# A four-layer graph network: layer 0 as the maximum of two rank-one terms, its denominator on TensorE, and half-row exponentials in layer 3

## The chip, the cores and the metric

The kernel runs on one core of a Trainium2 chip. The metric is the device time in microseconds (us), the median of three runs for the kernel before: 1418.75 us (1417.5 to 1420.33). PE is TensorE, DVE VectorE, ACT ScalarE, POOL GpSimd, SP the engine whose queue starts most of the transfers.

## The reference

There are N = 2708 nodes with 128 features each, and a dense 0/1 adjacency `adj` with ones on its diagonal. Four layers follow one another, each `x = x + layer(relu(layernorm(x)))`.

- Layer 0 (attention): `H = h W^T`; each node has two scores, `src` and `dst`; `Tau = adj^T * exp(max(0.2 C, C))` with `C = src[j] + dst[i]`; rows of `Tau` are divided by their sum; `Z = (adj^T * att) H`.
- Layer 1: normalised aggregation with `adj + I`, then a weight and a Relu.
- Layer 2: mean aggregation with `adj^T`, two weights, batch normalisation over the nodes, Relu.
- Layer 3 (attention over a dense product): `den = exp(leaky_relu(s_row + s_col))`, `num = adj den`, `att = den / num`, `H = adj (att XW)`.

All is float32.

## The kernel before, in words

The nodes are cut into T = 22 tiles of 128 rows, the last with 20. A row of 2708 columns is worked in two halves of 1354 (`HALF`) and, on PE, in six blocks of about 452 (`BLK`)[...]. Six banks (`acc_bank`) hold accumulators; two more (`bank`) go round for everything else.

Layer 0 (L212 to L261). The layernorm, the transposes (`relu_transposed`), a row of the `dst` scores spread over all partitions (`spread_row` into `row_a`, a plain copy) and the projection (`project` into `hs`, whose column 128 is the `src` score) come first. Then, for each tile and half, ACT adds the tile's score to the row (L228) and sums the row of the adjacency for the degree (L229), DVE forms the leaky maximum (L230), ACT takes the exponential (L231), DVE multiplies by the adjacency (L232, `tau`) and once more (L237, `at2`), POOL adds `tau` into `row_b` (L236), and PE aggregates `at2` into the six accumulators (L240). After the loop 22 small products against ones (L249) turn `row_b` into the denominator; the accumulators are copied out (`evacuate`), transposed, and added to `xs` scaled by its reciprocal (L258, L259).

Layers 1 and 2 (L274 to L345) stream the adjacency, transposed or not, through PE (`aggregate`, L192).

Layer 3 sorts the nodes by score and works in NS = 42 steps of 128 rows (L676 to L694). In a step three gathers on POOL's queue bring rows and values (`fetch`, L653); DVE forms the exponent `e` (L681); for each of the six blocks PE forms the product `num` (L685), ACT its logarithm (L686); DVE subtracts it from `e` in three pieces, after blocks 2, 4 and 5 (L688); one exponential over the whole row follows (L690). PE then adds the step before into the accumulators (`spread_values`, L674). `num` has only the two rotating banks; `e` and `ln` have two buffers.

The program is not ordered by hand. A planner writes the queue of each engine ahead of time, from the order of the program as priority and its own model of which instruction is ready; on the chip each engine then runs its queue in that order. What loads an activation table on ACT is placed afterwards, where the queue needs another table. Buffers of a pool are handed on when their last reader is done: four for the streamed adjacency, two for `z`, `tau` and `at2`.

At entry, ACT's queue starts the loads of `x` (one transfer of 1344 KB and a tail), then five weights, then eight vectors of 128 values, each scattered one value to a partition (`vecs`); SP's queue starts the adjacency.

Of the kernel before, what the change touches and what calls it, by code (L numbers as in the profile page):

```python
# [8 lines left out]
F32 = mybir.dt.float32  # L9
BF16 = mybir.dt.bfloat16  # L10
I32 = mybir.dt.int32
AF = mybir.ActivationFunctionType
# [5 lines left out]
def kernel(  # L18
# [19 lines left out]
    nc = tc.nc  # L38
# [11 lines left out]
    NB = len(BLK)  # L50
    NSTREAM, NKEEP = 4, 3

    def rows(t):
        return min(P, N - t * P)

    def cols(t):
        return slice(t * P, (t + 1) * P)

    def vcols(t):
        return slice(t * P, t * P + rows(t))  # L60
# [8 lines left out]
    def bank():  # L69
        return ps.tile([P, 512], F32, tag="bank", name="bank")  # L70

    def acc_bank(b):
        return ps_acc.tile([P, 512], F32, tag=f"acc{b}", name=f"acc{b}")
# [1 line left out]

    xs = big.tile([P, T, D], F32, name="xs")
    nc.vector.memset(xs[:, TF:, :], 0.0)
    nc.scalar.dma_start(xs[:, :TF, :], x[: TF * P, :].rearrange("(t p) d -> p t d", p=P))
    nc.scalar.dma_start(xs[:TAIL, TF, :], x[TF * P :, :])

    ident = const.tile([P, P], F32, name="ident")
    make_identity(nc, ident)
# [6 lines left out]
    def load(name, shape, src):  # L89
        t = const.tile(shape, F32, name=name)  # L90
        nc.scalar.dma_start(t, src)
        return t
# [3 lines left out]
    wn_sb = load("wn_sb", [P, P], w_n)  # L96
    wc_sb = load("wc_sb", [P, P], w_c)
    w3_sb = load("w3_sb", [P, P], w3)
    vecs = const.tile([P, 8], F32, name="vecs")
    for i, v in enumerate((att_src[0], att_dst[0], a3[0, :P], a3[0, P:], b_n, b_c, gamma, beta)):  # L100
        nc.scalar.dma_start(vecs[:, i : i + 1], v.rearrange("(p o) -> p o", o=1))

    def transposed(name, w):
        p = bank()
# [70 lines left out]
    def spread_row(dst, lhsT):  # L175

        for c in range(0, NPAD, 512):
            n = min(512, NPAD - c)
            p = bank()
            nc.tensor.matmul(p[:, :n], lhsT, hT[:, c : c + n], start=True, stop=True)  # L180
            nc.scalar.copy(dst[:, c : c + n], p[:, :n])

    def evacuate(b, acc):
        lo, hi = BLK[b]
# [11 lines left out]
    with tc.tile_pool(name="stream", bufs=NSTREAM) as stream, tc.tile_pool(name="keep", bufs=1) as keep, tc.tile_pool(  # L196
# [12 lines left out]
            return a  # L209


        layernorm()  # L212
        relu_transposed()
        spread_row(row_a, w0_spread[:, 1, :])
        project(w0_ext)
        deg2 = const.tile([P, T, 2], F32, name="deg2")
        nc.gpsimd.memset(deg2, 0.0)
        accs = [acc_bank(b) for b in range(NB)]
        for t in range(T):
            r = rows(t)  # L220
            a = load_rows(adj, t)
            for h in range(2):
                c = slice(h * HALF, (h + 1) * HALF)
                z = edge.tile([P, HALF], F32, tag="z", name="z")
                tau = edge.tile([P, HALF], F32, tag="tau", name="tau")
                at2 = edge.tile([P, HALF], F32, tag="at2", name="at2")
                junk = edge.tile([P, HALF], F32, tag="junk", name="junk", bufs=1)
                nc.scalar.activation(z[:r], row_a[:r, c], AF.Identity, bias=hs[:r, t, P : P + 1])  # L228
                nc.scalar.activation(junk[:r], a[:r, c], AF.Identity, accum_out=deg2[:r, t, h : h + 1])  # L229
                nc.vector.scalar_tensor_tensor(z[:r], z[:r], 0.2, z[:r], ALU.mult, ALU.max)  # L230
                nc.scalar.activation(z[:r], z[:r], AF.Exp)  # L231
                nc.vector.tensor_mul(tau[:r], a[:r, c], z[:r])  # L232
                if t == 0:
                    nc.gpsimd.tensor_copy(row_b[:, c], tau)
                else:
                    nc.gpsimd.tensor_add(row_b[:r, c], row_b[:r, c], tau[:r])  # L236
                nc.vector.tensor_mul(at2[:r], a[:r, c], tau[:r])  # L237
                for b in range(3 * h, 3 * h + 3):
                    lo, hi = BLK[b]
                    nc.tensor.matmul(  # L240
                        accs[b][:, : hi - lo],
                        hs[:r, t, :P],
                        at2[:r, lo - h * HALF : hi - h * HALF],
                        start=(t == 0),
                        stop=(t == T - 1),
                    )
        den = bank()
        for t in range(T):
            nc.tensor.matmul(den[: rows(t), t : t + 1], row_b[:, vcols(t)], ones[:, 0:1], start=True, stop=True)  # L249
        rden = small.tile([P, T], F32, tag="rden", name="rden")  # L250
        nc.vector.reciprocal(rden[:, :TF], den[:, :TF])
        nc.vector.reciprocal(rden[:TAIL, TF:], den[:TAIL, TF:T])
        for b in range(NB):
            evacuate(b, accs[b])
        for t in range(T):
            r = rows(t)
            p = bank()
            nc.tensor.transpose(p[:, :P], yT[:, cols(t)], ident)  # L258
            nc.vector.scalar_tensor_tensor(  # L259
                xs[:r, t, :], p[:r, :P], rden[:r, t : t + 1], xs[:r, t, :], ALU.mult, ALU.add  # L260
            )  # L261

        deg = const.tile([P, T], F32, name="deg")
        nc.vector.tensor_add(deg, deg2[:, :, 0], deg2[:, :, 1])
        deg1 = const.tile([P, T], F32, name="deg1")
        nc.vector.tensor_scalar_add(deg1, deg, 1.0)
        dis = const.tile([P, T], F32, name="dis")
# [55 lines left out]
        nc.vector.tensor_reduce(tot[:, 0:1], sums[:, 0, :], AX.X, ALU.add)  # L323
        nc.vector.tensor_scalar_mul(tot[:, 1:2], tot[:, 0:1], -1.0 / N)
        for b, (lo, hi) in enumerate(BLK):
            junk = edge.tile([P, HALF], F32, tag="junk", name="junk", bufs=1)
            nc.scalar.activation(
                junk[:, : hi - lo],
                row_b[:, lo:hi],
                AF.Square,  # L330
                bias=tot[:, 1:2],
                accum_out=sums[:, 1, b : b + 1],
            )
# [316 lines left out]
    with tc.tile_pool(name="att", bufs=2) as attp:  # L650

        def gather(out, src, idx):
            nc.gpsimd.indirect_dma_start(  # L653
                out=out,
                out_offset=None,
                in_=src,
                in_offset=bass.IndirectOffsetOnAxis(ap=idx, axis=0),
            )

        accs = [acc_bank(b) for b in range(NB)]  # L660
        done = {}

        def fetch(s):
            a = steps.tile([P, N], F32, tag="rows", name="rows")
            gather(a[:CH, :], adj_t[:, :], row_i[:CH, s : s + 1])
            gather(a[CH:, :], pre_d[:, :], pre_i[0:2, s : s + 1])
            xw = attp.tile([P, P], F32, tag="xw", name="xw", bufs=4)
            gather(xw, xw_d[:, :], xw_i[:, s : s + 1])
            return a, xw

        def spread_values(s):
            xw, e = done.pop(s)
            for b, (lo, hi) in enumerate(BLK):
                nc.tensor.matmul(accs[b][:, : hi - lo], xw, e[:, lo:hi], start=(s == 0), stop=(s == NS - 1))  # L674

        for s in range(NS):  # L676
            a, xw = fetch(s)
            nc.vector.tensor_scalar_mul(xw, xw, c_exp[:, s : s + 1])
            e = attp.tile([P, N], F32, tag="e", name="e")
            ln = attp.tile([P, N], F32, tag="ln", name="ln")  # L680
            nc.vector.tensor_scalar(e, row_a[:, :N], c_rel[:, s : s + 1], 0.0, ALU.add, ALU.max)  # L681
            beg = 0
            for b, (lo, hi) in enumerate(BLK):
                num = bank()
                nc.tensor.matmul(num[:, : hi - lo], dmat[:, s, :], a[:, lo:hi], start=True, stop=True)  # L685
                nc.scalar.activation(ln[:, lo:hi], num[:, : hi - lo], AF.Ln, bias=tiny)  # L686
                if b in (2, 4, 5):
                    nc.vector.tensor_sub(e[:, beg:hi], e[:, beg:hi], ln[:, beg:hi])  # L688
                    beg = hi
            nc.scalar.activation(e, e, AF.Exp)  # L690
            done[s] = (xw, e)
            if s:
                spread_values(s - 1)
        spread_values(NS - 1)  # L694
        for b in range(NB):
            evacuate(b, accs[b])


        scale = small.tile([P, T], F32, tag="scale", name="scale")
        nc.vector.scalar_tensor_tensor(scale, deg, 0.0, r_exp, ALU.not_equal, ALU.mult)  # L700
        for t0 in range(0, T, 4):
            n = min(4, T - t0)
            p = bank()
            for t in range(t0, t0 + n):
                nc.tensor.transpose(p[:, cols(t - t0)], yT[:, cols(t)], ident)
            for t in range(t0, t0 + n):
                nc.vector.tensor_scalar_mul(hn[:, t, :], p[:, cols(t - t0)], scale[:, t : t + 1])


        accs = [acc_bank(b) for b in range(NB)]  # L710
        for t in range(T):
            r = rows(t)
            a = stream_rows(adj_t, t)
            aggregate(t, hn[:r, t, :], a[:r], accs)
        for b in range(NB):
            evacuate(b, accs[b])
# [38 lines left out]
```

## Time and profile before

| | us |
|---|---|
| median of three runs | 1418.75 |
| the profiled execution | 1420.33 |
| its span, first to last instruction | 1418.5 |
| PE busy in the span | 1118.0 |
| DVE busy | 756.3 |
| ACT busy | 608.5 |
| POOL busy | 397.0 |
| layer 0, first to last aggregation on PE (L240) | 61.37 to 375.4 |
| layer 3 loop, about | 870 to 1292 |

The profile is of one execution. A line of a group reads: line, engine, operation, output<-inputs, shape, count, then the busy time in us and the mean of one in ns, then the time that the engine stood before these instructions and what released it. A line of the order of time reads: start, duration, engine, line, operation, and in brackets the idle time ahead of it. A line of a window reads: window, its length, busy time of PE, PEld (weight loads), DVE, ACT, POOL with counts, the granted TensorE clock as a share of full speed, the DMA engines' busy share, and GB/s.

### The profile page before, as it was taken

What the parts mean: (1) busy time and instruction counts of PE and PEld (TensorE: products, weight loads), DVE (VectorE), ACT (ScalarE), POOL (GpSimd) and SP (SyncE); (2) the same over time, 40 slices, a digit from 0 to 9 for tenths busy, and PEclk for the clock granted to TensorE, in tenths of its full rate; (3) what the DMA queues carried; (4) which work ended last, traced back from release to release, by engine and by line L of the source; (5) the groups of instructions that cost most, each with busy time, mean ns of one, the idle gap of its engine ahead of it and who ended that gap; (6) DMA issues with size and microseconds to landing.
All of it is one profiled execution on the core that took longest, in us unless ns stands there. A gap on an engine that the chain in (4) does not pass through costs nothing.

```text
span 1418.5 us, 8891 instructions
## 1 busy us (share of the span) xinstructions
PE 1118.0 (79%) x3090; PEld 539.9 (38%) x3090; DVE 756.3 (53%) x1078; ACT 608.5 (43%) x692; POOL 397.0 (28%) x191
## 2 busy tenths in 40 slices
PE   1644445454779988997668894999999999999998
PEld 1322222122534554543424441444444444444453
DVE  3699999999630052003595483445444555454002
ACT  2656565643000040003100014888888888885000
POOL 1265656565210001000100004454545444430000
PEclk9977777767579978996698897999999999999997
DMA  8123232321048734833102865334343544452882
GB/s 289 40 78 117 78 118 78 118 78 39 0 145 301 270 112 165 307 116 157 41 1 88 351 248 202 114 134 162 126 162 130 176 146 149 139 162 106 299 307 79
DMA packets 33210, 210.26 MB, mean 148 GB/s; under 512 B 6734, under 2 KB 13182, under 8 KB 14526
## 3 DMA queue, kind: packets, MB, share of 16 engines
q1 hardware_dynamic: 18336, 145.55, 28.1%
q0 software_dynamic: 9408, 61.00, 12.9%
q10 hardware_dynamic: 5422, 3.16, 0.8%
q8 instruction: 24, 0.39, 0.1%
q14 instruction: 20, 0.16, 0.0%
HBM read 206.38 MB, written 3.30 MB: 148 GB/s over the span
## 4 chain that ended last, share of the span: by engine, by line
PE 36%; issue 17%; POOL 14%; DVE 9%; ACT 1%; DMA 0%; POOLq 0%; DVEq 0%; ACTq 0%
PE acc L192 22%; POOL rows L653 7%; POOL xw L653 6%; PE acc L490 3%; DVE bits L446 1%; DVE bits L448 1%; DVE at L237 1%; DVE z L230 1%; POOL rstd L140 1%; PE bank L162 1%; PE bank L289 1%; PE bank L296 1%; PE bank L622 1%; PE acc L240 1%; PE acc L674 1%
## 5 line engine op out<-in xcount | busy, mean ns | idle before, releaser
L240 PE MATMUL acc<-at,hs 128*128 128x452 f32 (+2 forms) x264 | 156.0, 759 | 148.7 <-DVE at L237 148.7
L685 PE MATMUL bank<-rows,dmat 128*128 128x452 f32 (+1 forms) x504 | 223.0, 568 | 33.7 <-ACT ln L686 19.8
L236 POOL TENSOR_TENSOR row_b<-row_b,tau 128x1354 f32<-128x1354 f32 (+1 forms) x42 | 171.8, 4108 | 126.4 <-DVE tau L232 126.4
L674 PE MATMUL acc<-e,xw 128*128 128x452 f32 (+1 forms) x504 | 198.8, 543 | 2.7 <-ACT e L690 2.7
L192 PE MATMUL acc<-a,hn 128*128 128x452 f32 (+2 forms) x492 | 191.9, 552 | 8.9 <-DVE hn L276 8.9
L688 DVE TENSOR_TENSOR e<-e,ln 128x1354 f32<-128x1354 f32 (+2 forms) x126 | 134.3, 1097 | 96.5 <-ACT ln L686 96.5
L686 ACT ACTIVATE ln<-bank,tiny 128x452 f32<-128x452 f32 (+1 forms) x252 | 156.1, 636 | 52.5 <-PE bank L685 42.0
L240 PEld LDWEIGHTS acc<-at,hs 128*128 128x128 f32 (+1 forms) x264 | 69.0, 272 | 233.8 <-DVE at L237 171.9
L237 DVE TENSOR_TENSOR at<-a,tau 128x1354 f32<-128x1354 f32 x38 | 154.3, 4099 | 0.0
L685 PEld LDWEIGHTS bank<-rows,dmat 128*128 128x128 f32 x504 | 86.2, 191 | 163.5 <-ACT ln L686 110.9
L192 PEld LDWEIGHTS acc<-a,hn 128*128 128x128 f32 (+1 forms) x492 | 94.7, 193 | 104.5 <-issue 95.1
L653 POOL DMA_INDIRECT xw<-xw_d,xw_i x42 | 89.9, 2140 | 157.7 <-PE acc L674 152.1
L674 PEld LDWEIGHTS acc<-e,xw 128*128 128x128 f32 x504 | 95.8, 190 | 99.6 <-issue 88.2
L681 DVE TENSOR_SCALAR e<-row_a,c_rel 128x2708 f32<-128x2708 f32 x42 | 68.5, 1630 | 108.9 <-PE acc L674 108.9
L653 POOL DMA_INDIRECT rows<-in_adj_t_dram,row_i x42 | 53.5, 1274 | 216.5 <-DVE z L632 165.0
L231 ACT ACTIVATE z<-z 128x1354 f32<-128x1354 f32 (+1 forms) x44 | 58.7, 1333 | 126.1 <-DVE z L230 123.0
L188 ACT COPY yT<-acc 128x452 f32<-128x452 f32 (+1 forms) x12 | 6.4, 536 | 237.3 <-PE acc L192 213.5
L690 ACT ACTIVATE e<-e 128x2708 f32<-128x2708 f32 x42 | 103.3, 2460 | 3.2 <-DVE e L688 2.7
L192 PE MATMUL acc<-rows,hn 128*128 128x452 f32 (+2 forms) x264 | 102.5, 548 | 0.1
L186 DVE COPY yT<-acc 128x452 f32<-128x452 f32 (+1 forms) x12 | 7.5, 628 | 124.1 <-PE acc L192 111.3
L140 POOL TENSOR_TENSOR rstd<-isq,neg_half 128x22 f32<-128x22 f32 x4 | 15.5, 3863 | 194.2 <-DVE isq L139 169.5
L192 PEld LDWEIGHTS acc<-rows,hn 128*128 128x128 f32 (+1 forms) x264 | 49.8, 190 | 49.2 <-issue 48.9
(225 smaller groups left out, 1197.3 us busy)
## 6 DMA issues: line engine op xcount, KB each, us to landing
rows<-in_adj_t_dram SPq DMA_DIRECT2D x42, 1354.0 KB, 6.9
a<-in_adj_dram SPq DMA_DIRECT2D x38, 1354.0 KB, 6.1
a<-in_adj_t_dram SPq DMA_DIRECT2D x21, 1354.0 KB, 7.0
keep<-in_adj_dram SPq DMA_DIRECT2D x2, 1354.0 KB, 9.2
xw_d<-hs ACTq DMA_DIRECT2D x1, 1408.0 KB
out_dram<-xs SPq DMA_DIRECT2D x21, 64.0 KB, 1.6
rows<-in_adj_t_dram,row_i POOLq DMA_INDIRECT x42
xw<-xw_d,xw_i POOLq DMA_INDIRECT x42
```

What stands on the lines that cost most here:

```text
L192: nc.tensor.matmul(accs[b][:, : hi - lo], stationary, moving[:, lo:hi], start=(t == 0), stop=(t == T - 1))
L231: nc.scalar.activation(z[:r], z[:r], AF.Exp)
L236: nc.gpsimd.tensor_add(row_b[:r, c], row_b[:r, c], tau[:r])
L237: nc.vector.tensor_mul(at2[:r], a[:r, c], tau[:r])
L240: nc.tensor.matmul(accs[b][:, : hi - lo], hs[:r, t, :P], at2[:r, lo - h * HALF : hi - h * HALF], start=(t == 0), stop=(t == T - 1),)
L653: nc.gpsimd.indirect_dma_start(out=out, out_offset=None, in_=src, in_offset=bass.IndirectOffsetOnAxis(ap=idx, axis=0),)
L674: nc.tensor.matmul(accs[b][:, : hi - lo], xw, e[:, lo:hi], start=(s == 0), stop=(s == NS - 1))
L681: nc.vector.tensor_scalar(e, row_a[:, :N], c_rel[:, s : s + 1], 0.0, ALU.add, ALU.max)
L685: nc.tensor.matmul(num[:, : hi - lo], dmat[:, s, :], a[:, lo:hi], start=True, stop=True)
L686: nc.scalar.activation(ln[:, lo:hi], num[:, : hi - lo], AF.Ln, bias=tiny)
L688: nc.vector.tensor_sub(e[:, beg:hi], e[:, beg:hi], ln[:, beg:hi])
L690: nc.scalar.activation(e, e, AF.Exp)
```

## The change

1. `x` is loaded in three pieces of seven tiles and a tail on SP's queue, ahead of the adjacency. The eight vectors go as rows of one tile (`vrow`), which PE transposes into `vecs`.
2. In layer 0, `exp(max(0.2 C, C))` divided by `exp(dst)`, which the normalisation cancels, is `max(e^src, e^(0.2 src) * e^(-0.8 dst))`. `spread_row` now stores `exp(-0.8 dst)`, and one Relu with a scale and a bias of each row, `Relu(row * e_lo - e_hi)`, plus `e_hi`, is the maximum. A fused DVE pass adds `e_hi` and multiplies by the adjacency; a second DVE pass multiplies by it again.
3. The denominator is summed on PE: a stationary with one column of ones (`pick`) puts the column sums of block b into row b of one bank. For tiles 0, 3, ... 18 the sum is put off and `tau` is added on DVE to the next tile's first. POOL does nothing in the loop. The bank is then transposed in four pieces. Blocks are now 512 wide (the last 148), the halves 1536 and 1172; `at2` lies in `yT` and `row_b` in turn. The degree is one pass over the row for each tile.
4. In layer 3, each half of the row has its three Ln, then one subtraction, then an exponential of 1354.
5. A scratch tile of layer 2 (`junk`) becomes bf16.

```diff
-    nc.scalar.dma_start(xs[:, :TF, :], x[: TF * P, :].rearrange("(t p) d -> p t d", p=P))
-    nc.scalar.dma_start(xs[:TAIL, TF, :], x[TF * P :, :])
+    for t0 in range(0, TF, 7):
+        t1 = min(t0 + 7, TF)
+        nc.sync.dma_start(
+            xs[:, t0:t1, :], x[t0 * P : t1 * P, :].rearrange("(t p) d -> p t d", p=P)
+        )
+    nc.sync.dma_start(xs[:TAIL, TF, :], x[TF * P :, :])
...
+    vrow = const.tile([8, P], F32, name="vrow")
+    for i, v in enumerate((att_src[0], att_dst[0], a3[0, :P], a3[0, P:], b_n, b_c, gamma, beta)):
+        nc.scalar.dma_start(vrow[i : i + 1, :], v.rearrange("(o p) -> o p", o=1))
     vecs = const.tile([P, 8], F32, name="vecs")
-    for i, v in enumerate((att_src[0], att_dst[0], a3[0, :P], a3[0, P:], b_n, b_c, gamma, beta)):
-        nc.scalar.dma_start(vecs[:, i : i + 1], v.rearrange("(p o) -> p o", o=1))
+    pv = bank()
+    nc.tensor.transpose(pv[:, :8], vrow, ident[:8, :8])
+    nc.vector.tensor_copy(vecs, pv[:, :8])
...
-            nc.scalar.copy(dst[:, c : c + n], p[:, :n])
+            nc.scalar.activation(dst[:, c : c + n], p[:, :n], AF.Exp, scale=-0.8)
...
+        nc.scalar.activation(e_hi, hs[:, :, P], AF.Exp)
+        nc.scalar.activation(e_lo, hs[:, :, P], AF.Exp, scale=0.2)
+        nc.vector.tensor_scalar_mul(e_neg, e_hi, -1.0)
...
+        den = bank()
+        ndone, held = 0, {}
         for t in range(T):
             r = rows(t)
             a = load_rows(adj, t)
...
+            merged = t % 3 == 0 and t + 1 < T - 1
+            for h, (h0, h1) in enumerate(((0, CUT), (CUT, N))):
+                w = h1 - h0
+                tau = edge.tile([P, w], F32, tag=f"tau{h}", name=f"tau{h}", bufs=3)
+                at2 = (yT, row_b)[t % 2][:, h0:h1]
+                nc.scalar.activation(
+                    tau[:r, :w], row_a[:r, h0:h1], AF.Relu, bias=e_neg[:r, t : t + 1], scale=e_lo[:r, t : t + 1]
+                )
+                nc.vector.scalar_tensor_tensor(
+                    tau[:r, :w], tau[:r, :w], e_hi[:r, t : t + 1], a[:r, h0:h1], ALU.add, ALU.mult
+                )
+                nc.vector.tensor_mul(at2[:r, :w], a[:r, h0:h1], tau[:r, :w])
+                if t % 3 == 1 and t < T - 1:
+                    nc.vector.tensor_add(tau[:r, :w], tau[:r, :w], held[h][:r, :w])
+                held[h] = tau
...
+                if not merged:
+                    for b in range(3 * h, 3 * h + 3):
+                        lo, hi = E0[b]
+                        nc.tensor.matmul(
+                            den[: len(E0), : hi - lo],
+                            pick[:r, b, :],
+                            tau[:r, lo - h0 : hi - h0],
+                            start=(ndone == 0),
+                            stop=(t == T - 1 and b == NB - 1),
+                        )
+                        ndone += 1
+            junk = hn.rearrange("p t d -> p (t d)")[:, :N]
+            nc.scalar.activation(junk[:r], a[:r, :], AF.Identity, accum_out=deg[:r, t : t + 1])
+        den_sb = small.tile([8, 512], F32, tag="den_sb", name="den_sb", bufs=1)
+        nc.vector.tensor_copy(den_sb[: len(E0)], den[: len(E0), :])
+        dent = bank()
+        for q in range(4):
+            nc.tensor.transpose(dent[:, q * 8 : q * 8 + len(E0)], den_sb[: len(E0), cols(q)], ident[: len(E0), : len(E0)])
...
-            beg = 0
-            for b, (lo, hi) in enumerate(BLK):
-                num = bank()
-                nc.tensor.matmul(num[:, : hi - lo], dmat[:, s, :], a[:, lo:hi], start=True, stop=True)
-                nc.scalar.activation(ln[:, lo:hi], num[:, : hi - lo], AF.Ln, bias=tiny)
-                if b in (2, 4, 5):
-                    nc.vector.tensor_sub(e[:, beg:hi], e[:, beg:hi], ln[:, beg:hi])
-                    beg = hi
-            nc.scalar.activation(e, e, AF.Exp)
+            for h in range(2):
+                for b in range(3 * h, 3 * h + 3):
+                    lo, hi = BLK[b]
+                    num = bank()
+                    nc.tensor.matmul(num[:, : hi - lo], dmat[:, s, :], a[:, lo:hi], start=True, stop=True)
+                    nc.scalar.activation(ln[:, lo:hi], num[:, : hi - lo], AF.Ln, bias=tiny)
+                c = slice(h * HALF, (h + 1) * HALF)
+                nc.vector.tensor_sub(e[:, c], e[:, c], ln[:, c])
+                nc.scalar.activation(e[:, c], e[:, c], AF.Exp)
```

More of the change, by code (lines that the diff above doesn't have):

```diff
@@ L51 @@
     NSTREAM, NKEEP = 4, 3
+    E0 = [(c, min(c + 512, N)) for c in range(0, N, 512)]
+    CUT = 3 * 512
     def rows(t):
@@ L215 @@
         project(w0_ext)
-        deg2 = const.tile([P, T, 2], F32, name="deg2")
-        nc.gpsimd.memset(deg2, 0.0)
+        e_hi = const.tile([P, T], F32, name="e_hi")
+        e_lo = const.tile([P, T], F32, name="e_lo")
+        e_neg = const.tile([P, T], F32, name="e_neg")
+        nc.scalar.activation(e_hi, hs[:, :, P], AF.Exp)
+        nc.scalar.activation(e_lo, hs[:, :, P], AF.Exp, scale=0.2)
+        nc.vector.tensor_scalar_mul(e_neg, e_hi, -1.0)
+        pick = const.tile([P, len(E0), len(E0)], F32, name="pick")
+        nc.vector.memset(pick, 0.0)
+        for b in range(len(E0)):
+            nc.vector.memset(pick[:, b, b : b + 1], 1.0)
+        deg = const.tile([P, T], F32, name="deg")
+        nc.gpsimd.memset(deg, 0.0)
         accs = [acc_bank(b) for b in range(NB)]
+        den = bank()
+        ndone, held = 0, {}
         for t in range(T):
@@ L221 @@
             a = load_rows(adj, t)
[L222 to L237, printed above, removed]
+            merged = t % 3 == 0 and t + 1 < T - 1
[13 more added lines that the diff above has]
+                held[h] = tau
                 for b in range(3 * h, 3 * h + 3):
-                    lo, hi = BLK[b]
+                    lo, hi = E0[b]
                     nc.tensor.matmul(
@@ L242 @@
                         hs[:r, t, :P],
-                        at2[:r, lo - h * HALF : hi - h * HALF],
+                        at2[:r, lo - h0 : hi - h0],
                         start=(t == 0),
@@ L246 @@
                     )
[L247 to L254, printed above, removed]
+                if not merged:
+                    for b in range(3 * h, 3 * h + 3):
+                        lo, hi = E0[b]
+                        nc.tensor.matmul(
[13 more added lines that the diff above has]
+            nc.tensor.transpose(dent[:, q * 8 : q * 8 + len(E0)], den_sb[: len(E0), cols(q)], ident[: len(E0), : len(E0)])
+        rden = small.tile([P, 4, 8], F32, tag="rden", name="rden", bufs=1)
+        nc.vector.reciprocal(rden[:, :, : len(E0)], dent[:, :32].rearrange("p (q b) -> p q b", b=8)[:, :, : len(E0)])
+        for b, (lo, hi) in enumerate(E0):
+            if b % 2:
+                nc.vector.tensor_copy(yT[:, lo:hi], accs[b][:, : hi - lo])
+            else:
+                nc.scalar.copy(yT[:, lo:hi], accs[b][:, : hi - lo])
         for t in range(T):
@@ L259 @@
             nc.vector.scalar_tensor_tensor(
-                xs[:r, t, :], p[:r, :P], rden[:r, t : t + 1], xs[:r, t, :], ALU.mult, ALU.add
+                xs[:r, t, :], p[:r, :P], rden[:r, t % 4, t // 4 : t // 4 + 1], xs[:r, t, :], ALU.mult, ALU.add
             )
-        deg = const.tile([P, T], F32, name="deg")
-        nc.vector.tensor_add(deg, deg2[:, :, 0], deg2[:, :, 1])
         deg1 = const.tile([P, T], F32, name="deg1")
@@ L325 @@
         for b, (lo, hi) in enumerate(BLK):
-            junk = edge.tile([P, HALF], F32, tag="junk", name="junk", bufs=1)
+            junk = edge.tile([P, BW], BF16, tag="junk", name="junk", bufs=1)
             nc.scalar.activation(
```

## The prediction

> **What bounds the kernel now.** I read the windows by stage first, then the groups of the layer 0 stage, then the order of time inside one step of the layer 3 loop. Windows (window, length, busy time of PE, PEld, DVE, ACT, POOL, clock, DMA share, GB/s):
>
> ```profile
> 57.00:352.00 295.00, 146.60 (x252) 65.21 (x252) 295.00 (x128) 164.35 (x156) 168.78 (x42) 0.74 0.25 89
> 890.00:1280.00 390.00, 372.09 (x931) 166.57 (x929) 194.72 (x194) 339.42 (x349) 181.90 (x112) 1.00 0.44 146
> 725.00:740.00 15.00, 9.90 (x44) 4.12 (x43) 15.00 (x29) 0.00 (x0) 0.00 (x0) 1.00 0.00 0
> ```
>
> Layer 0 (57 to 352) is VectorE's: busy all 295 us, 14.19 us a tile from one L230 to the next (92.22, 106.41, 120.60). The layer 3 loop is PE's and ACT's together: 372 and 339 of 390 us, 9.98 us a step. Groups of layer 0:
>
> ```profile
> L236 POOL TENSOR_TENSOR row_b<-row_b,tau 128x1354 f32<-128x1354 f32 x40 | 163.6, 4108 | 120.4 <-DVE tau L232 120.4
> L237 DVE TENSOR_TENSOR at<-a,tau 128x1354 f32<-128x1354 f32 x38 | 154.3, 4099 | 0.0
> L230 DVE SCALAR_TENSOR_TENSOR z<-z 128x1354 f32<-128x1354 f32 x40 | 60.7, 1556 | 0.0
> L232 DVE TENSOR_TENSOR tau<-a,z 128x1354 f32<-128x1354 f32 x38 | 58.1, 1569 | 0.0
> ```
>
> L237 and L232 are the same product of the same shape, 4.10 against 1.57 us: L237 runs beside POOL's 4.11 us addition, L232 doesn't. One layer 3 step in order of time (start, duration):
>
> ```profile
> 993.98 1.28 ACT L686 ACT_TABLE_LOAD   x1
> 995.27 1.17 ACT L686 ACTIVATE ln<-bank,tiny 128x452 f32<-128x452 f32 x2
> 997.02 1.40 ACT L686 ACTIVATE ln<-bank,tiny 128x450 f32<-128x450 f32 x2 [0.58 <-PE bank L685]
> 997.69 1.57 DVE L688 TENSOR_TENSOR e<-e,ln 128x1354 f32<-128x1354 f32 x1 [1.96 <-ACT ln L686]
> 998.78 1.39 ACT L686 ACTIVATE ln<-bank,tiny 128x452 f32<-128x452 f32 x2 [0.35 <-PE bank L685]
> 1000.19 1.28 ACT L690 ACT_TABLE_LOAD   x1
> 1001.48 2.46 ACT L690 ACTIVATE e<-e 128x2708 f32<-128x2708 f32 x1
> ```
>
> ACT closes the step: loads 2.57, Ln 3.96, Exp 2.46, waits 0.93. Ln and Exp each bring a load.
>
> **What the Trainium skill says.** "ScalarE: Activation LUTs", section What ACT_TABLE_LOAD costs: about 1283 ns plus a drain of about 1380; here 1.28 and no drain (Exp starts 1.30 us after the last Ln ends). Its section Table sets says that Ln and Exp share a set; the trace disagrees, 42 loads at each line. "SBUF — State Buffer", Who interferes with whom: a VectorE instruction with two SBUF inputs is blocked by a GpSimd one that reads SBUF; L237 agrees. "TensorE: Matmul & The Clock Gate", Part 1: an idle window of about 3.4 us halves the clock. The trace agrees in kind (clock is the third last number):
>
> ```profile
> 880.00:882.70 2.70, 0.10 (x1) 0.00 (x0) 0.00 (x0) 2.69 (x2) 0.45 (x1) 1.00 0.79 281
> 882.70:884.00 1.30, 1.03 (x2) 0.30 (x2) 0.00 (x0) 1.28 (x2) 0.00 (x0) 0.92 0.90 358
> 884.00:887.50 3.50, 2.70 (x4) 1.27 (x5) 1.57 (x1) 1.90 (x4) 0.00 (x0) 0.50 0.08 31
> 887.50:890.50 3.00, 3.00 (x5) 1.47 (x5) 1.22 (x2) 1.40 (x3) 0.00 (x0) 0.50 0.00 0
> ```
>
> About 2.7 us of idle, one short burst, then 6.8 us at half clock; while gaps under 1 us (725 to 740, PE 66% busy) keep 1.00.
>
> **The change, part by part.** Entry: VectorE's first L148 waits to 14.88 for x. Now x goes in four pieces, ahead of the adjacency on SP's queue: 1.4 MB at the 289 GB/s of the first slice is 4.8 us. L148/L149 take 22 x 0.26 us. The eight vector rows queue behind five weights on ACT's queue (13 issues x 0.45 = 5.9 us, landing 5.1), so the transpose of vrow, and VectorE behind its copy, may stand until 11 to 14 us. POOL's 3.9 us power follows; hn starts near 20, not 30.84. From hn to PE's first aggregation: 30.5 us before. Now all of hs and e_hi, e_lo, e_neg must be there before the first Relu, about 6 us later than the first L228 was (48.97 against the last L173 near 55), but from there to PE it is Relu 1.7, two passes of 1.75, where L228 to L240 took 12.4: -7. I call it unchanged. Sum -10 (bounds 0 and -15).
>
> Loop: VectorE per tile has two passes of 2708 (2 x 3.1) and in 7 tiles an addition (3.1): 22 x 6.2 + 7 x 3.1 = 158 us. POOL has nothing, so L237's 2.5 us of blocking goes. ACT: Relu 2.85 + degree pass 2.65 = 5.5 a tile. PE: the old six aggregations plus six one-hot sums in 15 tiles (7 are merged into the next): 37 rows; a row took 105.28/22 = 4.79 us in layer 1 (clock 0.95) and 12 matmuls took 4.71 in layer 3. 37 x 4.7 = 174, plus 5 for a cold start and handoffs: 179. PE sets it. The narrow stationary is in no row of before: at worst the full 4.7; a gain is excluded, since all 2708 columns still stream. Before, first to last aggregation (L240) ran from 61.37 to 375.4: 314 us, with the 9.28 us of L249 in it, now gone; what is late next, after VectorE, is PE itself. Sum -135 (-122 to -142).
>
> Tail: copy of den 0.6, four transposes about 1.5, reciprocal 0.3, all behind the last sum: +2. The evacuations hide behind them. Layer 0 in all: -143.
>
> Layer 3, 42 steps. Program order now has three Ln, a subtraction, half an Exp, twice. Behind the first half Exp, waiting for its subtraction, stand three Ln, so two banks, so PE. The framework's planner orders by readiness (in layer 0 it wrote L228 of both halves before either L231), so I expect it to move the fourth and fifth Ln, whose products come 0.75 us apart, ahead of the first Exp; the sixth, later than the subtraction, stays behind it. Then ACT changes table four times, not two. One step laid end to end from the rows above: Ln 0.6 each with the two waits on banks, five done at 4.1; load to 5.4; Exp of 1354 (L231: 1.33) to 6.7; load to 8.0; Ln to 8.6; load, hiding all but 0.3 of the subtraction 1.57, to 10.3; Exp to 11.6; load to 12.9. That is +2.9. The same layout of the old order gives 9.92, against 9.98 measured. In the new layout PE has both banks filled and the step before added at 10.4, and stands 3.2 us until the next step's first Ln frees a bank: longer than the gap above. If the clock halves, the products cost 1.5 instead of 0.75 and the fifth Ln and all behind it come 0.7 or more later; a step near 13.65 us, four of the 3.4 us windows, would meet the window at the same place again. I take 13.65: 42 x 3.67 = +154 (bounds: +0.1 a step if the sixth Ln goes ahead too; +5.7 if the clock stays low).
>
> At nothing I cost: the gathers (POOL issues them three steps ahead and waits for PE, 152 us of idle at L653, so a longer step only relaxes them); the memsets for pick, in VectorE's idle first 14.88 us, without that cover about 1 us (six at 0.17); the bf16 junk tile at L326, same columns through ACT; and the adjacency loads of layer 0, which land about 5 us later behind x but are first read some 35 us after that. In the loop a tile's load lands 6.1 us after its issue, four buffers deep, against 8 us a tile: hidden.
>
> Sum: 1418.5 - 143 + 154 = 1429.5 span; that execution took 1420.33, 1.8 above its span and 1.6 above the median: about 1430.
>
> **Rivals.** (B) The clock holds in layer 3: 12.5 to 13.0 us a step, +106 to +127, so 1382 to 1403, faster. For it: 725 to 740 at 66% busy; against it: the 3.2 us gap. It decides at 143/42 = 3.4: below 13.4 us a step the kernel is faster. (C) The planner puts all six Ln first: the change to layer 3 doesn't do what it says, two loads, +4, so 1279. Only 0.2 us separate the sixth Ln from the Exp in the layout. (D) Deeper cold, 14.3 to 15.7 a step: 1457 to 1516. (E) In layer 0 PE and VectorE (174 and 158) wait for each other over two at2 buffers: 9.2 us a tile, about 25 more, 1445 to 1470.
>
> **How the numbers follow.** My case 46% (1408 to 1452), B 24%, C 8%, D 13%, E 9%. The range 1376 to 1484 leaves out C and the upper half of D. Within 0.2% (2.8 us, about what three runs can tell) 6%. Faster: B, C and the low end of mine, 36%; slower 58%.
>
> **What would show it.** Layer 0 at 8 us a tile with PE over 90% busy, the product at 1.5 us; 168 table loads in the layer 3 loop, 13 to 14 us a step, clock below 1.00 there. 84 loads, or a clock of 1.00 at under 13.4 us, would prove me wrong.

## The result and the profile after

The changed kernel takes 1459.45 us (median of four runs, 1455.63 to 1459.94), the kernel before 1418.12 in the runs beside it (1414.41 to 1420.33): a ratio of 1.0288, 95% interval 1.026 to 1.0317. It is slower, as forecast, and by more: +41.3 us where +11 was said. The profiled execution of the changed kernel took 1459.76 us, with a span of 1458.0.

Marks that both traces have split the difference of the two spans, 39.5 us:

| from, to | before | after | difference |
|---|---|---|---|
| start to the power ahead of layer 1 (rstd on POOL) | 390.76 | 251.81 | -138.95 |
| to the first product of layer 3 (`num` on PE) | 479.15 | 477.19 | -1.96 |
| to the start of the last aggregation of layer 3 | 430.6 | 610.2 | +179.6 |
| to the end of the span | 118.0 | 118.8 | +0.8 |

So one stage gained almost what was forecast, another lost more, and nothing else moved by more than 2 us. Part 5 lies in the second stage, which shows no loss; it has no run of its own. The windows of the two stages after the change:

```profile
57.00:247.00 190.00, 188.53 (x465) 64.42 (x464) 158.32 (x145) 102.14 (x77) 4.03 (x1) 0.94 0.37 134
890.00:1330.00 440.00, 345.61 (x729) 156.65 (x729) 148.03 (x120) 347.72 (x364) 126.04 (x82) 0.85 0.31 102
```

In the first line VectorE, busy without a break before, has 158 of 190 us, and PE has taken its place at the limit with 188.5. In the second, PE fell from 95% busy (372 of 390 us) to 79% (346 of 440), and the clock from 1.00 to 0.85. The groups of layer 0 after:

```profile
L274 PE MATMUL bank<-tau,pick 128*6 128x512 f32 x140 | 64.7, 592 | 0.1
L264 PE MATMUL acc<-yT,hs 128*128 128x512 f32 x103 | 48.6, 606 | 0.0
...
L255 DVE SCALAR_TENSOR_TENSOR tau<-tau,e_hi,a 128x1536 f32<-128x1536 f32 x17 | 30.8, 1810 | 1.6 <-ACT tau L252 1.6
...
L258 DVE TENSOR_TENSOR row_b<-a,tau 128x1536 f32<-128x1536 f32 x9 | 15.7, 1750 | 0.4 <-PE acc L264 0.4
```

The second product, L237 with 4.10 us for 1354 columns, is now L258 with 1.75 for 1536. A sum with the one-hot stationary of six columns costs what a full aggregation does, 592 against 606 ns. The PE groups have next to no idle time ahead of them (0.1 us).

One step of layer 3 after, in order of time:

```profile
1002.95 1.28 ACT L726 ACT_TABLE_LOAD   x1
1004.25 1.17 ACT L726 ACTIVATE ln<-bank,tiny 128x452 f32<-128x452 f32 x2
1004.94 6.20 PE L725 MATMUL bank<-rows,dmat 128*128 128x450 f32 x8 [3.18 <-ACT ln L726]
1006.84 0.64 ACT L726 ACTIVATE ln<-bank,tiny 128x450 f32<-128x450 f32 x1 [1.43 <-PE bank L725]
...
1008.35 0.64 ACT L726 ACTIVATE ln<-bank,tiny 128x452 f32<-128x452 f32 x1 [0.87 <-PE bank L725]
...
1009.86 0.64 ACT L726 ACTIVATE ln<-bank,tiny 128x452 f32<-128x452 f32 x1 [0.87 <-PE bank L725]
1010.51 1.28 ACT L729 ACT_TABLE_LOAD   x1
1010.98 4.71 PE L713 MATMUL acc<-e,xw 128*128 128x452 f32 x12
1011.81 1.33 ACT L729 ACTIVATE e<-e 128x1354 f32<-128x1354 f32 x1
1013.16 1.28 ACT L726 ACT_TABLE_LOAD   x1
1014.45 0.64 ACT L726 ACTIVATE ln<-bank,tiny 128x450 f32<-128x450 f32 x1
1015.11 1.28 ACT L729 ACT_TABLE_LOAD   x1
...
1016.73 1.33 ACT L729 ACTIVATE e<-e 128x1354 f32<-128x1354 f32 x1 [0.33 <-DVE e L728]
```

Five Ln, a load, half an Exp, a load, the sixth Ln, a load, the other half: four loads a step. PE stands 3.18 us until the step's first Ln frees a bank; its next four products (eight matmuls in the trace) take 6.20 us, and three Ln wait for them 1.43, 0.87 and 0.87 us, 3.17 in all. In the step of the kernel before, the Ln waited 0.93 us, and the same four products took 3.53 behind a gap of 0.38:

```profile
995.97 3.53 PE L685 MATMUL bank<-rows,dmat 128*128 128x450 f32 x8 [0.38 <-ACT ln L686]
```

The clock (third last number) in three windows of the step after the change:

```profile
1000.00:1004.90 4.90, 1.76 (x5) 0.57 (x3) 3.11 (x2) 4.54 (x5) 3.77 (x3) 0.91 0.06 13
1004.90:1007.00 2.10, 2.06 (x3) 1.17 (x4) 0.00 (x0) 0.67 (x2) 0.81 (x1) 0.50 0.75 201
1007.00:1011.00 4.00, 4.00 (x7) 1.60 (x6) 1.76 (x2) 2.25 (x4) 0.00 (x0) 0.52 0.58 241
```

PE is busy without a pause from 1004.94, and yet has half the clock until about 1011. This step is the longest of four kinds that take turns: from one load ahead of its first Ln to the next, steps take 15.12, 14.16, 14.48 and 14.30 us. In the other three the four products take about 5 us, and the Ln wait 2.2 to 2.5. Windows laid at the changes of the clock, over these four steps, show why:

```profile
1004.01:1010.83 6.82, 5.89 (x8) 2.76 (x9) 1.76 (x2) 3.62 (x7) 1.40 (x2) 0.50 0.59 208
1010.83:1021.07 10.24, 7.39 (x20) 3.48 (x19) 3.11 (x2) 9.28 (x9) 4.25 (x3) 1.00 0.11 21
1021.07:1024.48 3.41, 3.41 (x6) 1.29 (x5) 1.76 (x2) 1.74 (x3) 0.00 (x0) 0.50 0.85 292
1024.48:1034.72 10.24, 7.14 (x20) 3.33 (x18) 3.11 (x2) 9.77 (x10) 4.23 (x3) 1.00 0.16 41
1034.72:1038.14 3.42, 3.42 (x6) 1.53 (x5) 1.77 (x2) 1.28 (x2) 0.27 (x1) 0.50 0.79 307
1038.14:1048.38 10.24, 7.13 (x19) 3.22 (x18) 3.11 (x2) 9.45 (x9) 3.95 (x2) 1.00 0.08 28
1048.38:1051.79 3.41, 3.10 (x4) 1.46 (x5) 0.52 (x1) 1.43 (x3) 0.86 (x1) 0.50 0.75 236
1051.79:1062.03 10.24, 8.02 (x21) 3.52 (x19) 4.35 (x4) 9.45 (x9) 3.15 (x2) 1.00 0.16 59
```

The lengths are 3.41 us or a multiple of it. This holds for the whole loop: the clock changes 79 times between 737.77 and 1328.27 us, and each change lies, to 0.01 us, a whole number of periods of 3.413 us after the first. In three steps of four the half clock lasts one period, in the fourth two. Four steps, 58.03 us, are 17 periods. Over the steady part a step takes 14.51 us (mean of the last 28), against 9.98.

### The profile page after: what moved, and what is told of

Read it like the earlier page. It is cut to its first block, busy times and chain, and to the rows that moved or that the text cites. A ratio compares the mean times of both kernels' runs of the same rounds, so it can differ in the third digit from the quotient of the medians.

```text
span 1458.0 us, 9096 instructions
## 1 busy us (share of the span) xinstructions
PE 1205.5 (83%) x3231; PEld 559.0 (38%) x3231; DVE 596.8 (41%) x1014; ACT 662.8 (45%) x731; POOL 210.0 (14%) x147
## 4 chain that ended last, share of the span: by engine, by line
PE 58%; ACT 26%; DVE 11%; issue 2%; DMA 1%; POOL 1%; ACTq 0%; POOLq 0%; DVEq 0%
PE acc L203 21%; PE bank L725 12%; ACT e L729 8%; PE acc L264 8%; ACT L726 7%; ACT ln L726 6%; PE bank L274 5%; DVE e L728 4%; ACT L729 4%; PE acc L529 3%; DVE bits L485 1%; PE bank L173 1%; POOL rstd L151 1%; PE bank L183 1%; PE bank L335 1%
## 5 line engine op out<-in xcount | busy, mean ns | idle before, releaser
L725 PE MATMUL bank<-rows,dmat 128*128 128x452 f32 (+1 forms) x504 | 292.8, 731 | 142.6 <-ACT ln L726 130.3
L728 DVE TENSOR_TENSOR e<-e,ln 128x1354 f32<-128x1354 f32 x84 | 131.9, 1570 | 396.7 <-ACT ln L726 396.7
L725 PEld LDWEIGHTS bank<-rows,dmat 128*128 128x128 f32 x504 | 118.3, 245 | 304.3 <-ACT ln L726 232.7
L726 ACT ACTIVATE ln<-bank,tiny 128x452 f32<-128x452 f32 (+1 forms) x252 | 155.8, 636 | 106.1 <-PE bank L725 104.1
L692 POOL DMA_INDIRECT xw<-xw_d,xw_i x42 | 105.8, 2518 | 293.8 <-PE acc L713 288.2
L729 ACT ACTIVATE e<-e 128x1354 f32<-128x1354 f32 x84 | 111.9, 1332 | 13.9 <-DVE e L728 13.4
L252 ACT ACTIVATE tau<-row_a,e_neg,e_lo 128x1536 f32<-128x1536 f32 (+3 forms) x44 | 65.1, 1510 | 35.8 <-PE bank L274 32.2
L274 PE MATMUL bank<-tau,pick 128*6 128x512 f32 (+1 forms) x180 | 75.5, 556 | 0.1
L203 PEld LDWEIGHTS acc<-rows,hn 128*128 128x128 f32 (+1 forms) x264 | 50.0, 191 | 49.4 <-issue 49.1
L255 DVE SCALAR_TENSOR_TENSOR tau<-tau,e_hi,a 128x1536 f32<-128x1536 f32 (+1 forms) x38 | 60.4, 1620 | 4.9 <-ACT tau L252 4.9
L264 PE MATMUL acc<-yT,hs 128*128 128x512 f32 x132 | 56.1, 567 | 7.5 <-DVE yT L258 7.5
L529 PE MATMUL acc<-rows,wts 128*44 128x452 f32 (+3 forms) x264 | 56.9, 578 | 2.8 <-issue 2.8
```

The lines of the kernel that those rows point to most:

```text
L203: nc.tensor.matmul(accs[b][:, : hi - lo], stationary, moving[:, lo:hi], start=(t == 0), stop=(t == T - 1))
L252: nc.scalar.activation(tau[:r, :w], row_a[:r, h0:h1], AF.Relu, bias=e_neg[:r, t : t + 1], scale=e_lo[:r, t : t + 1])
L264: nc.tensor.matmul(accs[b][:, : hi - lo], hs[:r, t, :P], at2[:r, lo - h0 : hi - h0], start=(t == 0), stop=(t == T - 1),)
L274: nc.tensor.matmul(den[: len(E0), : hi - lo], pick[:r, b, :], tau[:r, lo - h0 : hi - h0], start=(ndone == 0), stop=(t == T - 1 and b == NB ...
L529: nc.tensor.matmul(accs[b][64 * h : 64 * h + 2 * NC, : hi - lo], wts[:r, t, :], a[:r, lo:hi], start=(t == 0), stop=(t == T - 1),)
L692: nc.gpsimd.indirect_dma_start(out=out, out_offset=None, in_=src, in_offset=bass.IndirectOffsetOnAxis(ap=idx, axis=0),)
```

## The experiments

**Theory.** The change is two: a new layer 0 worth about -139, and part 4, worth +180. Part 4 costs that because ACT changes tables four times a step, and because the gap that this leaves on PE halves the clock just when the next step's products are wanted. **Rivals:** the half rows and their waits cost, not the loads; the low clock is a by-product that other work hides; layer 0 is not set by PE; its gain is the fused Relu's and not POOL's.

**Part 4 taken out, and part 4 alone.** The first is the changed kernel with the loop of before; the second the kernel before with the new loop (the diff is the reverse).

```diff
-            for h in range(2):
-                for b in range(3 * h, 3 * h + 3):
...
-                nc.scalar.activation(e[:, c], e[:, c], AF.Exp)
+            for b, (lo, hi) in enumerate(BLK):
...
+            nc.scalar.activation(e, e, AF.Exp)
```

> The changed kernel with the layer 3 loop of before (part 4 undone). Theory: parts 1 to 3 save the 139 us read in the two traces and part 4 alone costs 180, so about 1279 us, with 84 table loads in the loop, 10.0 us a step and a clock of 1.00 there. Rival: the earlier start of layers 1 to 3 or the buffers of the new layer 0 cost the loop something too: 1300 us or more.

Measured: 1279.38 us (1278.1 to 1280.23), ratio to before 0.9013 (0.8998 to 0.9028); steady steps of 9.98 us, clock 1.00. This version beats both kernels.

> The kernel before with part 4 alone. Theory: the loop costs the same 180 us whatever stands ahead of it, so about 1598 us, 14.5 us a step, clock 0.85 in the loop. Rival: the slow steps hang on when the loop meets the clock's windows, so that another start gives another size: 1545 (12.9 us a step) to 1660.

Measured: 1595.13 us (1594.04 to 1597.02), ratio 1.1239 (1.1221 to 1.1258); 14.50 us a step, clock 0.86. The two parts add to within 8 us: 140.9 less and 174.8 more, each against the 1420.29 of before beside them, make 33.9 where 41.3 was measured. Part 4 costs 174.8 in the kernel before and 180.1 on top of the rest; the start at another time changed the size by some 5 us at most. A window of the loop in each of the two:

```profile
800.00:1000.00 200.00, 191.84 (x481) 86.04 (x480) 101.10 (x100) 174.60 (x181) 98.75 (x61) 1.00 0.43 147
900.00:1400.00 500.00, 391.39 (x833) 177.14 (x831) 170.00 (x140) 399.34 (x416) 158.62 (x104) 0.86 0.31 102
```

**The gap on PE filled.** Short matmuls with nothing to do with the result (60 columns of the accumulators' banks that nobody reads) stand in PE's queue behind the second product of each step. The kernel computes the same.

```diff
+            nums = []
...
+                    nums.append(nc.tensor.matmul(num[:, : hi - lo], dmat[:, s, :], a[:, lo:hi], start=True, stop=True))
+                    if s > 1 and b == 1:
+                        with tc.issue_after(nums[1].ins):
+                            for q in range(8):
+                                nc.tensor.matmul(
+                                    accs[q % NB][:, 452:512], dmat[:, s, :], a[:, :60], start=False, stop=False
+                                )
```

> The changed kernel with eight short matmuls of 60 columns on unused columns of the accumulators behind the second product of every step, to fill PE's 3.2 us gap. Theory: the low clock is what makes a step 14.5 instead of 12.9 us, so the clock stays near 1.00 in the loop and 42 x 1.6 us come back: about 1392 us, in spite of the added work. Rival: the loads and waits on ACT alone set the step, and the low clock is hidden: 1459 us or more.

Measured: 1427.12 us (1416.58 to 1427.25), ratio 1.0052 (1.0035 to 1.0068). That is 32 us less than the changed kernel, for 320 matmuls more, so the rival, a hidden clock, falls; but the forecast 1392 was missed, and the clock was 0.94, not 1.00. The windows say why (clock third last):

```profile
1013.50:1019.00 5.50, 5.50 (x16) 2.81 (x15) 0.92 (x2) 5.42 (x6) 2.34 (x3) 1.00 0.53 181
1019.00:1023.20 4.20, 2.51 (x20) 2.00 (x18) 2.35 (x2) 3.83 (x5) 2.46 (x1) 0.96 0.31 111
1023.20:1028.00 4.80, 4.80 (x8) 2.11 (x9) 1.77 (x2) 2.45 (x5) 0.00 (x0) 0.68 0.00 0
```

Eight fillers last 1.9 us and leave 1.5 to 1.7 of the gap. After that, in every second step, the clock still falls: steps of 13.02 and 14.29 us take turns. The profiled execution, 1416.58, was the shortest of the five, and the others were near 1427 at a lower mean clock (0.904 to 0.908 over the span against 0.917), so they may have had more such steps; no trace of them shows it. Next, fourteen fillers, 3.2 us of work.

```diff
-                            for q in range(8):
+                            for q in range(14):
```

> The run before with fourteen short matmuls in place of eight. There eight filled 1.9 us of the gap, 1.5 to 1.7 us stayed open, and some steps ran at the low clock (0.93 to 0.95 over the loop), others took 13.0 us. Theory: fourteen fill 3.3 us, the clock stays 1.00, every step takes 12.9 to 13.1 us: 1459 less 42 x 1.45 = about 1398 us. Rival: the eight that are there already give all that the clock takes, and the rest is queueing: 1417 to 1427 us again, or slower by the added 1.4 us a step.

Measured: 1403.2 us (1402.18 to 1405.88), ratio 0.9906 (0.9871 to 0.9942): 0.9% faster than the kernel before. Two hundred us of the loop, and one step in order of time:

```profile
900.00:1100.00 200.00, 194.74 (x811) 117.37 (x810) 76.25 (x62) 177.07 (x185) 75.14 (x46) 1.00 0.35 114
```

```profile
1004.71 1.68 PE L726 MATMUL bank<-rows,dmat 128*128 128x452 f32 x4
...
1006.23 3.23 PE L730 MATMUL acc<-rows,dmat 128*128 128x60 f32 x28
...
1007.83 1.28 ACT L733 ACT_TABLE_LOAD   x1
1009.12 1.17 ACT L733 ACTIVATE ln<-bank,tiny 128x452 f32<-128x452 f32 x2
1009.81 3.53 PE L726 MATMUL bank<-rows,dmat 128*128 128x450 f32 x8 [0.35 <-ACT ln L733]
1010.87 1.40 ACT L733 ACTIVATE ln<-bank,tiny 128x450 f32<-128x450 f32 x2 [0.58 <-PE bank L726]
```

The fillers (L730) close the gap to 0.35 us, the four products behind them take 3.53 us and not 5 to 6.20, the clock is 1.00 from 737.27 us, in the loop's first step, to its last aggregation at 1283.2, and every steady step takes 13.02 us. The four loads a step are all still there. What is left of the loss, 13.02 against 9.98, is theirs or the half rows'.

**The same halves, but the Ln held in front.** Here both half exponentials stay, and are kept behind all six Ln of their step in ACT's queue.

```diff
+                last = nc.scalar.activation(ln[:, lo:hi], num[:, : hi - lo], AF.Ln, bias=tiny)
...
+            with tc.issue_after(last.ins):
+                for h in range(2):
+                    c = slice(h * HALF, (h + 1) * HALF)
+                    nc.scalar.activation(e[:, c], e[:, c], AF.Exp)
```

> The changed kernel with the two half-row exponentials of part 4, but both held behind all six Ln of their step in ACT's queue. Theory: the split of the row is harmless and the four alternations are the cost: two loads a step, 10.0 to 10.2 us a step, clock 1.00, about 1280 to 1288 us. Rival: the halves themselves (two subtractions of half a row, an exponential that waits for the second) cost: over 11 us a step, above 1320 us.

Measured: 1284.77 us (1280.92 to 1286.16), ratio 0.9057 (0.9023 to 0.9091); 10.07 us a step, clock 1.00. ACT's queue in one step:

```profile
1001.57 1.17 ACT L724 ACTIVATE ln<-bank,tiny 128x452 f32<-128x452 f32 x2
1003.32 1.40 ACT L724 ACTIVATE ln<-bank,tiny 128x450 f32<-128x450 f32 x2 [0.58 <-PE bank L723]
1005.07 1.40 ACT L724 ACTIVATE ln<-bank,tiny 128x452 f32<-128x452 f32 x2 [0.35 <-PE bank L723]
1006.49 1.28 ACT L731 ACT_TABLE_LOAD   x1
1007.78 2.55 ACT L731 ACTIVATE e<-e 128x1354 f32<-128x1354 f32 x2
1010.35 1.28 ACT L724 ACT_TABLE_LOAD   x1
```

Splitting the row costs 0.09 us a step. The order in ACT's queue costs the rest.

**No table to change.** Square stands in place of Exp in the loop, so the exponential is left out; the order of the queue is that of the changed kernel.

```diff
-                nc.scalar.activation(e[:, c], e[:, c], AF.Exp)
+                nc.scalar.activation(e[:, c], e[:, c], AF.Square)
```

> The changed kernel with Square in place of Exp in the layer 3 loop (leaves out the exponential), in the same order of ACT's queue: no table load is left in the loop. Theory: four loads of 1.28 us are what opens the gap, so a step falls to 9.1 to 10 us at a clock of 1.00: about 1250 to 1285 us. Rival: the wait of a half row's activation for its subtraction, with the Ln queued behind it, is the cause: over 12 us a step, above 1370 us.

Measured: 1258.01 us (1255.64 to 1259.62), 9.57 us a step. With the alternation of activations kept and the loads gone, PE is busy all the time:

```profile
800.00:900.00 100.00, 100.00 (x253) 44.24 (x251) 52.58 (x43) 64.56 (x83) 47.27 (x31) 1.00 0.45 155
```

The wait of a half for its subtraction, with Ln queued behind it, is the rival that falls. From the first product to the start of the last matmul of the aggregation, the loops put the loss in order:

| loop of layer 3 | us | step |
|---|---|---|
| Square for Exp, no loads | 407.1 | 9.57 |
| kernel before, two loads | 430.6 | 9.98 |
| half rows, Ln in front, two loads | 435.2 | 10.07 |
| half rows, four loads, gap filled | 549.6 | 13.02 |
| the same, gap half filled | 575.1 | 13.65 (mean) |
| changed kernel, gap open | 610.2 | 14.51 (mean) |

The times are those of the profiled executions; that of the half-filled gap was 10.5 us below its kernel's median. Of the 179.6 us, 4.6 go to the halves, 114.4 to the two further loads with what waits on them, and 60.6 to the clock. The split between the last two rests on the run with fourteen fillers; as the products behind them still wait for a Ln, the fillers themselves cost the loop next to nothing.

**Layer 0: what sets it.** First the column sums of all 22 tiles on PE and no addition on VectorE.

```diff
-            merged = t % 3 == 0 and t + 1 < T - 1
+            merged = False
...
-                if t % 3 == 1 and t < T - 1:
+                if False:
```

> The changed kernel with the column sums of all 22 tiles on TensorE and no addition on VectorE. Theory: TensorE sets layer 0's loop at 4.7 us a row of six, so seven rows more cost 33 us: about 1492 us. Rival: VectorE or the handoff of the two product buffers sets it: 1459 or less, since VectorE loses 7 x 3.1 us.

Measured: 1491.2 us (1489.32 to 1492.54), 31.8 above the changed kernel: 4.5 us for each of the seven rows more, while VectorE had seven additions less. PE sets the loop. The other way round, eight tiles merged in place of seven, on top of the layer 3 loop of before:

```diff
-            merged = t % 3 == 0 and t + 1 < T - 1
+            merged = t % 5 in (0, 2) and t < 20
...
-                if t % 3 == 1 and t < T - 1:
+                if t % 5 in (1, 3) and t < 20:
```

> The changed layer 0 with the layer 3 loop of before, and eight tiles (0, 2, 5, 7, 10, 12, 15, 17) in place of seven whose column sums are put off and added on VectorE. Theory: TensorE alone sets the loop, so one row less of six sums is 4.7 us: about 1275 us against the 1279 without it. Rival: at 161 us VectorE is close enough that the two wait for each other: 1279 or more.

Measured: 1276.45 us (1274.21 to 1278.67), ratio 0.8996 (0.8981 to 0.9011) against 0.9013 (0.8998 to 0.9028) with seven. The intervals overlap, so 2.9 us of the expected 4.7 is not told from nothing. In the two traces the power ahead of layer 1 comes at 247.48 and 251.31 us, 3.8 earlier with eight, and PE is busy all 178 us from 52 to 230 in both; one execution of each is not enough to settle the size.

**Layer 0: POOL's part.** The kernel before without POOL's additions, and so without the denominator, which is one constant.

```diff
                 if t == 0:
-                    nc.gpsimd.tensor_copy(row_b[:, c], tau)
-                else:
-                    nc.gpsimd.tensor_add(row_b[:r, c], row_b[:r, c], tau[:r])
+                    nc.gpsimd.memset(row_b[:, c], 1.0)
```

> The kernel before without the 22 x 2 additions on GpSimd in layer 0 (leaves out the denominator, which is set to one column of ones). Theory: they are what makes the second product take 4.10 us instead of 1.57, so the tile falls from 14.2 to about 9.2 us: some 110 us less, about 1308 us, and most of part 2 and 3 of the change would be had by taking GpSimd off the loop. Rival: the second product is slow by itself or VectorE then waits for ACT: 1390 us or more.

Measured: 1299.11 us (1297.04 to 1299.88), 119.5 below before. The second product in the groups of the loop (here L235, the first is L232), and a window of it:

```profile
L235 DVE TENSOR_TENSOR at<-a,tau 128x1354 f32<-128x1354 f32 x38 | 57.8, 1561 | 0.0
...
L232 DVE TENSOR_TENSOR tau<-a,z 128x1354 f32<-128x1354 f32 x37 | 56.4, 1566 | 0.8 <-ACT z L231 0.8
```

```profile
57.00:240.00 183.00, 123.23 (x271) 57.50 (x271) 182.19 (x126) 161.26 (x154) 0.00 (x0) 0.86 0.40 144
```

The two products now cost the same, 1.56 us; VectorE is still the bound. This kernel pays nothing for the denominator, so 119.5 is not what such a change could bring, but it shows how much of layer 0's gain is POOL's absence.

**The entry alone.** The kernel before with part 1.

```diff
-    nc.scalar.dma_start(xs[:, :TF, :], x[: TF * P, :].rearrange("(t p) d -> p t d", p=P))
-    nc.scalar.dma_start(xs[:TAIL, TF, :], x[TF * P :, :])
+    for t0 in range(0, TF, 7):
+        t1 = min(t0 + 7, TF)
+        nc.sync.dma_start(
...
+        nc.scalar.dma_start(vrow[i : i + 1, :], v.rearrange("(o p) -> o p", o=1))
...
+    nc.tensor.transpose(pv[:, :8], vrow, ident[:8, :8])
+    nc.vector.tensor_copy(vecs, pv[:, :8])
```

> The kernel before with part 1 alone (x in pieces on SP's queue, the eight vectors as rows, transposed on TensorE). Theory: hn is ready near 20.7 instead of 30.84 us and all behind it keeps that, so 9 to 10 us less, about 1409 us. Rival: the first aggregation then waits for something else (the adjacency behind x, the projection) and less than half arrives: 1414 us or more.

Measured: 1402.54 us (1401.48 to 1410.35, five runs), ratio 0.989 (0.9876 to 0.9904): 14 to 18 us less, more than expected. In its trace the first aggregation is at 49.4 us, not 61.37, and the power ahead of layer 1 at 378.76, not 390.76: -12.0, of which 9.9 are left in the span. That execution was the longest of the five, with the lowest mean clock (0.870 against 0.873 to 0.878); where the other four found some 5 to 9 us more was not seen.

## Why the prediction was right, and where it was wrong

- **Entry, -10.** The first `hn` came at 20.68 (20 was said, 30.84 before), and PE's first aggregation 9.5 us earlier. Right in the changed kernel; alone, the part was worth more.
- **Loop of layer 0, -135.** From the first aggregation at 51.86 to the end of the last column sum at 234.98 it took 183.1 us, against 314: -131, inside the bounds. PE set it, as said, at 99% busy; the 179 was short by 4. The blocking by POOL, that bore 2.5 us of each second product, holds by the run without POOL's additions. Rival E, the handoff, falls: all the second products together wait 2.5 us for PE in the whole loop, and PE next to nothing for them. The prediction says that a narrow stationary is in no row of before; L490 there has one of 44 columns, at 587 ns for 452 columns moved, against 549 for L192 with 128. It would have given the same answer.
- **Tail, +2.** From the end of the last sum to the power 16.8 us, before 15.4: +1.5. In all -138.95 where -143 was said.
- **The order of layer 3.** The planner did what was said: the fourth and fifth Ln ahead of the first half exponential, the sixth behind; 84 loads at L726 and 84 at L729. Rival C falls with that. The warm layout of 12.9 us a step stands at 13.02 in the run with the gap filled, and PE's gap of 3.2 at 3.18.
- **The step that failed** is "I take 13.65" in the sum of layer 3: the surcharge of the low clock on the warm step, "0.7 or more", was mis-sized. The mechanism, a halved clock after the gap, was right. The working lets one product cost 1.5 us instead of 0.75 and moves what follows by that. In the trace the half clock lasts one period of 3.41 us in three steps of four, and two in the fourth. The four products behind the gap then take 5 to 6.20 us in place of 3.53, and the Ln wait 2.2 to 3.2 in place of 0.93. The surcharge is 1.14 to 1.46 us in the steps with one low period and 2.10 in the step with two: 1.49 on the mean and not 0.75, 60.6 us in the loop and not 32. The warm part was nearly right, 119 us over the loop (549.6 less 430.6) where 42 x 2.92 = 123 was said; its small error and the 4 us that layer 0 fell short all but cancel.
- **The period.** The idea that the loop meets fixed windows was right: the clock changes only on the grid of 3.413 us. A step of four such windows did not come about, since one low window already costs more than the 0.63 us that 13.65 leaves above 13.02. Instead four steps fill 17 windows, 14.51 us a step; with eight fillers two steps, 13.02 and 14.29, fill eight. The sum then is that of rival D, 14.3 to 15.7 us a step, 1457 to 1516. That the kernel is slower hung on this one term: with nothing for the clock, 13.02 us a step, the whole would have come out faster, as in the run with the gap filled.
- **Rival B** had its place too: at 13.02 us a step, under its 13.4, the kernel with the filled gap is faster than before, 0.9906: with the clock held the whole change is a gain of 1%.

## What to carry to other kernels

Count the table loads in the order that ACT's queue will have, not in the order of the program: an activation that is split to start earlier can put a load on each side of both its halves. Price a gap on TensorE by what runs at half speed after it and by who waits for that, not by its length; and if the gap can't be removed, try to fill it with short matmuls that nobody reads, and look whether enough of them stand there, since eight left two fifths of what the clock cost (25.5 of 60.6 us) and fourteen none. When a change has parts in different stages, cost and run them apart: here the better half alone is 10% faster than before, and the whole 3% slower.

## What was not expected of the hardware

- 560 matmuls without use made the kernel 56 us faster (1459.45 to 1403.2), though they took PE's time in a loop where PE is at the limit's edge (97% busy with them).
- The clock changes on a fixed grid: all 79 changes in the loop of layer 3 lie whole multiples of 3.413 us apart. In windows of this grid, in the changed kernel, the half clock followed each of the 39 windows at full clock in which PE was busy 39% or less, and none of the 85 with 46% or more. From half clock it came back after each of the 39 windows with PE busy 84% or more, and after none of the 10 with 68 to 76%.
- The busy share is not all of it. With eight fillers, a gap of 1.7 us behind 1.9 us of them dropped the clock in every second step, after windows that the profile calls 61 to 67% busy. A gap of 1.5 in the steps between, cut by the grid at another place, did not, nor did gaps of 0.35 us with fourteen. What share of which work holds the clock is not shown.
- A column sum with a stationary of six columns took 592 ns for 512 columns, a full one of 128 took 606: its narrowness brought nothing here.
